# Three engines take the loop's instructions in the order of the source: an attention and feed-forward layer on one core

## The chip, the core and the metric

The kernel runs on one core of a Trainium2 chip. A core has a matrix engine (TensorE, PE in the profile; PEld is its weight load), a vector engine (VectorE, DVE), an activation engine (ScalarE, ACT), a general engine (GpSimd, POOL) and a queue that issues most transfers (SyncE, SP). Each engine takes its own instructions strictly in the order in which they stand in the built program, and waits at its head for what that instruction needs. The metric is the time of one execution in microseconds.

## The reference, cut to what matters

The input is 8 sequences of 1024 rows of width 256. Each goes through attention with 16 heads of 16, whose scores get a fixed band ("prior") added, then a layer norm, then a feed-forward part with ternary weights and a squared ReLU, then a second layer norm.

```python
scores = jnp.einsum('bhqd,bhkd->bhqk', Q, K) / math.sqrt(hd)
scores = scores + prior_lambda * _gaussian_mask(Lx)[None, None, :, :]
attn = jax.nn.softmax(scores, axis=-1)
out = jnp.einsum('bhqk,bhkd->bhqd', attn, V)
...
h = _bitlinear(x, w_fc) + gate * (x @ v.T @ fast_b.T @ u.T)
r = jnp.maximum(h, 0.0)
return _bitlinear(r * r, w_proj)
...
x = _layernorm(x + _L0_attn_ref(x, ...), axis=-1)
x = _layernorm(x + _L0_ffn_ref(x, ...), axis=-1)
```

All of it is in fp32; the queries and keys are split into two parts so that a faster fp32 form gives full precision.

## The kernel before

The heads are worked in groups of four. For each group the scores are computed twice: once with the queries on the partitions, to find each row's maximum (tiles `s`), and once with the keys on the partitions (tiles `e`), where the maxima, negated, come in as two more rows of the contraction. `exp` of `e` goes to SBUF, and a third product with the values gives the weighted sums (tile `av`).

The main loop has 512 turns, numbered by `g`, after 11 turns that only fill the pipeline. What one turn puts into the source, in this order:

- **E** (`exp_scores`, L437 to L462): two tiles `e`, each of two matmuls (L449), called E0 and E1 here. DVE adds the prior in place (L459) in the part of the tile that the band reaches; ACT takes `exp` (L461). Of each 8 turns in a row two have adds of 488 elements, two of 372, one of 116 and three have none.
- The second maximum that the turn before left over (`max_row`, L398 to L409: one DVE instruction over 1024 elements, L401).
- Every eighth turn `set_max` (L412 to L435): the maxima of a step are transposed on PE (`pmx`, L417), negated by two DVE instructions (`both`) and sent through DRAM into the query tiles, two turns before they are needed.
- **J**: two steps of the side work. Side jobs are Python generators in one queue (`jobs_of`, `run_job`): the projections of the next heads or the next sequence, the preparation of the weights, and the output projection and feed-forward part of the sequence before, in `chunk`s of 256 rows. A job hands control back at each `yield`.
- **S** (`max_scores`, L376 to L396): four matmuls for the scores 11 turns ahead. Tiles `s_0` and `s_1` are written alternately, one from the upper half of the array's rows and one from the lower half. DVE takes the maximum of `s_0` at once and that of `s_1` in the next turn.
- **AV** (`weigh`, L467 to L499): four matmuls with the `exp` of the turn before. Each has 17 output rows, in its own quarter of the array's columns. At the end of a step of 8 turns DVE and ACT copy `av` out (`avs`, L487, each taking two of the four heads) and it goes to DRAM; at the end of a sequence `normalize` (L502 to L521) reads the sums back, inverts them on DVE (L507) and scales.

The PSUM memory holds three tiles for `s` and `e` together (pool `ps_se`), one for `av`, and one, `misc`, for all side work. So E1 of a turn reuses the place of the `s_0` of the turn before; S needs the place of the turn's own E0 (free after its `exp`) and that of the `s_1` of the turn before (free after its maximum). Each side product must wait until the one before it has been taken out of `misc`: `ph` by ACT (`rl`, L591), `ptx1` by ACT (L574), `pk` and `pq` by ACT (`full`, L347), `po` and `py` by DVE (L562, L607), which then goes on with a layer norm (L523 to L541). In it POOL computes one small power (L532) for which DVE waits.

The order in the built program isn't that of the source. A scheduler takes the instructions at build time, prefers earlier source, and passes over what isn't ready by its own reckoning of durations: a matmul whose place in PSUM isn't free yet lets later ones pass. In the order built for the kernel before, the 2048 matmuls of AV stand in 913 groups with other matmuls between them (388 groups of one, 83 of two, 294 of three, 133 of four), those of S in 840 groups, of which 265 hold two of the upper half alone and 252 two of the lower half alone, and those of E in 833.

Of the kernel before, what the change touches and what calls it, by code (L numbers as in the profile page):

```python
# [10 lines left out]
F32 = mybir.dt.float32  # L11
# [5 lines left out]
P = 128  # L17
# [19 lines left out]
def tile_postln_layer(  # L37
# [20 lines left out]
    nc = tc.nc  # L58
    B, L, D = x.shape
# [19 lines left out]
    p1 = ctx.enter_context(tc.tile_pool(name="p1", bufs=1))  # L79
# [17 lines left out]
    def big(name):  # L97
        return epool.tile([P, 2 * HALF], F32, tag="e", name=name)
# [11 lines left out]
    for name, w in (("q", wq), ("k", wk), ("v", wv), ("o", wo)):  # L110
        t = big(f"raw_{name}")[:, : NDC * D].rearrange("p (c d) -> p c d", d=D)
# [4 lines left out]
    for name, src in (("q", bq), ("k", bk)):  # L116
        t = cpool.tile([P, NDC], F32, tag=f"b{name}", name=f"b{name}")
# [57 lines left out]
    for name in ("q", "k", "v"):  # L175
        t = cpool.tile([P, NDC, D], F32, tag=f"w{name}T", name=f"w{name}T")
# [20 lines left out]
    for s in range(SLOTS):  # L197
        for pr in range(NP):
            for a in range(2):
                for name in "qk":  # L200
                    t = cpool.tile(
                        [P, L], F32R, tag=f"{name}{s}{pr}{a}", name=f"st_{name}_{s}_{pr}_{a}"
                    )
# [7 lines left out]
    for n in range(2):  # L211
        t = cpool.tile([P, NB, NH, VW], F32, tag=f"v{n}", name=f"v_{n}")
# [7 lines left out]
    def ternary(w, n, name):  # L220

        sc = p2.tile([P, 3], F32, tag="sc", name=f"sc_{name}")
        t = big(f"tern_{name}")[:, :n]
        nc.vector.tensor_reduce(
            out=sc[:, 0:1], in_=w, axis=AX.X, op=ALU.add, apply_absolute_value=True
        )
        nc.vector.tensor_scalar(sc[:, 0:1], sc[:, 0:1], 1.0 / n, 1e-5, op0=ALU.mult, op1=ALU.max)
        nc.vector.tensor_scalar_mul(sc[:, 1:2], sc[:, 0:1], 0.5)  # L230
        nc.vector.tensor_scalar_mul(sc[:, 2:3], sc[:, 0:1], -0.5)
        nc.vector.tensor_scalar(t, w, sc[:, 1:2], None, op0=ALU.is_gt)
        nc.vector.scalar_tensor_tensor(
            out=t, in0=w, scalar=sc[:, 2:3], in1=t, op0=ALU.is_lt, op1=ALU.subtract
        )
        nc.vector.tensor_add(t, t, w)
        nc.vector.tensor_sub(t, w, t)
        nc.vector.tensor_scalar_mul(w, t, sc[:, 0:1])
# [3 lines left out]
    def prepare_fc(i):  # L242

        w = p1.tile([P, FF], F32, tag="rT", name=f"fc_{i}")[:, :D]
        nc.sync.dma_start(w, w_fc[ts(i, P), :])
        yield False
        ternary(w, D, f"fc_{i}")
        pu = misc(f"pu_{i}")
        nc.tensor.matmul(pu[:R, :P], u_sb[:, i, :], ident, start=True, stop=True)
        uT = p2.tile([R, P], F32, tag="uT", name=f"uT_{i}")  # L250
        nc.vector.tensor_copy(uT, pu[:R, :P])
        yield False
        pa = misc(f"pa_{i}")
        nc.tensor.matmul(pa[:R, :P], fb_sb, uT, start=True, stop=True)
        a = p2.tile([R, P], F32, tag="a", name=f"a_{i}")
        nc.vector.tensor_scalar_mul(a, pa[:R, :P], gate_c)
        yield False
        pw = misc(f"pw_{i}")
        for dc in range(NDC):
            nc.tensor.transpose(pw[:, ts(dc, P)], w[:, ts(dc, P)], ident)  # L260
        nc.vector.tensor_copy(wfT[:, :, ts(i, P)], pw[:, :D].rearrange("p (c h) -> p c h", h=P))
        yield False
        pl = misc(f"pl_{i}")
        for dc in range(NDC):
            nc.tensor.matmul(pl[:, ts(dc, P)], v_sb[:, ts(dc, P)], a, start=True, stop=True)
        nc.vector.tensor_add(
            wfT[:, :, ts(i, P)], wfT[:, :, ts(i, P)], pl[:, :D].rearrange("p (c h) -> p c h", h=P)
        )
        yield False

    def prepare_proj(i):
        w = p1.tile([P, FF], F32, tag="rT", name=f"proj_{i}")
        nc.sync.dma_start(w, w_proj[ts(i, P), :])
        yield False
        ternary(w, FF, f"proj_{i}")
        yield False
        for q in range(NHC // 4):
            pw = misc(f"pp_{i}_{q}")
            for c in range(4):
                nc.tensor.transpose(pw[:, ts(c, P)], w[:, ts(4 * q + c, P)], ident)  # L280
            nc.scalar.copy(wpT[:, ts(q, 4), ts(i, P)], pw.rearrange("p (c h) -> p c h", h=P))
            yield False
# [77 lines left out]
    def fill_stack(G):  # L360

        (b, g), s = divmod(G, NG), G % SLOTS
        for pr in range(NP):
            for a in range(2):
                at = P // 2 * a
                src = HD * ((g % 2) * HG + 2 * pr + a)
                for name in "kq":
                    nc.sync.dma_start(
                        stack[name, s, pr, a][at : at + P // 2].bitcast(F32),
                        parts_of[name, b, g // 2][src : src + HD].rearrange("p l n -> (p l) n"),  # L370
                    )
# [284 lines left out]
    for G in range(SLOTS):  # L656
        fill_stack(G)

    total = B * PER_B // 2
    opened, rest, es = False, None, {}  # L660
    for g in range(-LEAD, total + 1):
# [30 lines left out]
    for c in range(NCH):  # L692
        for _ in chunk(B - 1, c):
            pass


# [45 lines left out]
```

## Time and profile before

| what | value |
|---|---|
| median of 3 runs | 3170.52 us (3157.24 to 3173.5) |
| the profiled execution's own time | 3172.75 us |
| its span, first to last instruction | 3170.7 us |
| PE busy | 2984.8 us, 94% |
| DVE busy | 1912.3 us, 60% |
| ACT busy | 1237.8 us, 39% |
| first `exp` of the loop, end of the last | 99.2 us, 3020.7 us |
| mean granted TensorE clock | 0.950 |

The times are of one execution, taken by the hardware profiler. A line of a group reads: source line, engine, operation, output<-inputs, shapes, count, then the busy time and the mean length of one in ns, then the idle time of the engine before these instructions and what ended it. A line of the timeline reads: start and length in us, engine, line, operation, and how many equal ones followed each other; in brackets, how long the engine was idle before it and what released it. The busy time of PE is a union of lengths whose ends are modelled, so the start of one matmul to the start of the next tells more than the length. A line of the stages reads: stage, its length, then for each engine the busy time and the number of instructions, then the granted clock, the share of the transfer engines and GB/s. The clock in the profile's rows is either 1.00 or 0.50 at any one time; the mean says how the time divides.

From the first `exp` to the last the loop takes 2920 us, 5.70 us a turn. Some 99 us stand before it (loads, weights, the first projections and the first 11 turns of S) and 151 us after it (the last sequence's normalization and its four chunks).

### The profile page before, as it was taken

Reading aid. Unit: us, or ns where it says so; the run is one execution under the profiler, and the core shown is the slowest. Engines: PE = TensorE matmul, PEld = TensorE weight load, DVE = VectorE, ACT = ScalarE, POOL = GpSimd, SP = SyncE. Lnnn points to the kernel's source line nnn. Section 1 sums busy time; section 2 is a strip of 40 time slices with the busy share of each in tenths; the row PEclk is TensorE's granted clock in tenths of the full one; section 3 lists DMA queues with packets and bytes.
Section 4 is the critical chain, followed back from the end, with each engine's and each line's share of the span. In section 5 each row is a group of like instructions: output and inputs, shape, how many; then the busy total and the mean of one; then the engine's idle time right before and its main releaser. Section 6 shows DMA issues by size and latency. Waiting matters only on the chain.

```text
span 3170.7 us, 33164 instructions
## 1 busy us (share of the span) xinstructions
PE 2984.8 (94%) x11440; PEld 1311.8 (41%) x11440; DVE 1912.3 (60%) x3675; ACT 1237.8 (39%) x1417; POOL 407.3 (13%) x451
## 2 busy tenths in 40 slices
PE   4999999999999999999999999999999999999956
PEld 2333334444344443444344443444434444444335
DVE  3667675665666666566556656656665665666511
ACT  0323443443444444343444434444343434444410
POOL 4000101111110111101111111101111011111011
PEclk7867999999999998999999999999999999999978
DMA  5112322031312303122221312222031222202000
GB/s 152 58 36 54 105 52 77 24 98 43 92 51 52 91 23 98 37 88 68 58 64 29 106 43 79 64 52 87 24 102 37 78 71 51 80 21 52 12 23 14
DMA packets 106568, 193.89 MB, mean 61 GB/s; under 512 B 19264, under 2 KB 47952, under 8 KB 106400
## 3 DMA queue, kind: packets, MB, share of 16 engines
q1 hardware_dynamic: 104992, 190.38, 21.4%
q8 instruction: 90, 1.47, 0.2%
q10 hardware_dynamic: 1088, 1.05, 0.1%
q14 instruction: 78, 0.64, 0.1%
q0 software_dynamic: 320, 0.35, 0.1%
HBM read 105.73 MB, written 85.98 MB: 60 GB/s over the span
## 4 chain that ended last, share of the span: by engine, by line
PE 77%; issue 8%; DVE 7%; ACT 5%; DMA 2%; POOL 2%; SPq 0%; ACTq 0%; DVEq 0%; POOLq 0%
PE av L473 24%; PE e L449 16%; PE s L389 15%; PE ph L581 8%; PE py L598 6%; ACT exp L461 3%; DVE junk L401 3%; PE pk L336 2%; PE pv L309 2%; PE pq L336 2%; DVE e L459 1%; PE po L553 1%; DVE r L534 1%; ACT rl L591 1%; ACT avs L487 1%
## 5 line engine op out<-in xcount | busy, mean ns | idle before, releaser
L401 DVE CUSTOM_DVE_ANT_0 junk<-s,wide 128x1024 f32<-128x1024 f32 x1024 | 1249.6, 1220 | 718.3 <-PE s L389 688.5
L461 ACT ACTIVATE exp<-e 128x1024 f32<-128x1024 f32 x1024 | 1015.9, 1022 | 1285.0 <-DVE e L459 869.7
L473 PE MATMUL av<-exp,v 128*17 128x512 f32 x4096 | 1002.9, 615 | 0.2 <-ACT exp L461 0.2
L449 PE MATMUL e<-st_q,st_k 66*128 66x512 f32 (+1 forms) x2048 | 751.2, 465 | 17.0 <-ACT exp L461 9.2
L389 PE MATMUL s<-st_k,st_q 64*128 64x512 f32 x2048 | 654.3, 464 | 72.0 <-ACT exp L461 43.6
L449 PEld LDWEIGHTS e<-st_q,st_k 66*128 66x128 f32 (+1 forms) x2048 | 360.1, 195 | 514.0 <-issue 262.0
L389 PEld LDWEIGHTS s<-st_k,st_q 64*128 64x128 f32 x2048 | 269.0, 191 | 556.6 <-ACT exp L461 236.5
L459 DVE TENSOR_TENSOR e<-e,wide 128x372 f32<-128x372 f32 (+2 forms) x640 | 335.0, 543 | 248.1 <-PE e L449 242.7
L581 PE MATMUL ph<-x1T,wfT 128*128 128x256 f32 x1024 | 283.9, 411 | 13.8 <-ACT rl L591 9.4
L598 PE MATMUL py<-wpT,rT 128*128 128x256 f32 x1024 | 257.9, 386 | 3.0 <-ACT rl L591 3.0
L473 PEld LDWEIGHTS av<-exp,v 128*17 128x17 f32 x4096 | 114.9, 96 | 342.9 <-issue 324.0
L581 PEld LDWEIGHTS ph<-x1T,wfT 128*128 128x128 f32 x1024 | 197.5, 201 | 103.1 <-ACT rl L591 46.0
L598 PEld LDWEIGHTS py<-wpT,rT 128*128 128x128 f32 x1024 | 188.4, 189 | 80.1 <-issue 48.0
L592 POOL TENSOR_TENSOR rT<-rl 128x512 f32<-128x512 f32 x128 | 133.0, 1039 | 642.2 <-ACT rl L591 642.2
L487 ACT COPY avs<-av 17x512 f32<-17x512 f32 x128 | 73.9, 577 | 208.8 <-DVE avs L487 207.5
L591 ACT ACTIVATE rl<-ph 128x512 f32<-128x512 f32 x128 | 76.8, 600 | 156.8 <-PE ph L581 156.8
L487 DVE COPY avs<-av 17x512 f32<-17x512 f32 x128 | 87.4, 683 | 82.3 <-PE av L473 59.3
L532 POOL TENSOR_TENSOR rstd<-ve,mhalf 128x2 f32<-128x2 f32 x64 | 44.4, 694 | 599.4 <-DVE ve L530 599.4
L349 POOL CAST twok<-fullk 128x512 fp32r<-128x512 f32 x32 | 19.5, 610 | 616.3 <-ACT fullk L347 485.6
L553 PE MATMUL po<-woT,o 128*128 128x256 f32 x256 | 74.2, 399 | 21.9 <-POOL o L520 18.5
L520 POOL TENSOR_TENSOR o<-o,rec 128x512 f32<-128x512 f32 x32 | 40.5, 1285 | 409.5 <-DMA rec<-back 409.4
L548 POOL TENSOR_TENSOR x<-x,bo_row 128x256 f32<-128x256 f32 x64 | 45.8, 736 | 345.5 <-DMA x<-in_L_attn_x_dram 330.8
(109 smaller groups left out, 1100.6 us busy)
## 6 DMA issues: line engine op xcount, KB each, us to landing
parts_k<-twok SPq DMA_DIRECT2D x64, 512.0 KB
st_k<-parts_k SPq DMA_DIRECT2D x128, 256.0 KB
st_q<-parts_q SPq DMA_DIRECT2D x128, 256.0 KB
parts_q<-twoq SPq DMA_DIRECT2D x32, 512.0 KB
parts_q<-twoq SPq DMA_DIRECT2D x64, 256.0 KB
x<-in_L_attn_x_dram SPq DMA_DIRECT2D x16, 512.0 KB
x<-in_L_attn_x_dram SPq DMA_DIRECT2D x32, 256.0 KB
raw_o<-avs SPq DMA_DIRECT2D x256, 32.0 KB
```

The costliest lines, as they stand in the source:

```text
L336: nc.tensor.matmul(pt, wT[name][:, dc, ts(c, P)], xT[:, dc, ts(half, HALF)], start=(dc == 0), stop=(dc == NDC - 1),)
L389: nc.tensor.matmul(pair[a][:, kh, :], stack["q", s, pr, a][rows, ts(blk, P)], stack["k", s, pr, a][rows, ts(kh, HALF)], start=True, stop=True,
L401: nc.vector.tensor_tensor_reduce(out=junk, in0=t.rearrange("p k n -> p (k n)"), in1=wide[:, LEFT - P * blk : LEFT - P * blk + L], scale=1. ...
L449: nc.tensor.matmul(t[:, a, :], stack["k", s, pr, a][rows, ts(blk, P)], stack["q", s, pr, a][rows, ts(h, HALF)], start=True, stop=True,)
L459: nc.vector.tensor_add(part, part, add)
L461: nc.scalar.activation(e, t.rearrange("p a n -> p (a n)"), AF.Exp)
L473: nc.tensor.matmul(av_of[step][32 * j : 32 * j + HD + 1, :], v_bufs[b % 2][:, blk, g * HG + j, : HD + 1], es[j // 2][:, ts(j % 2, HALF)], ...
L487: (nc.scalar.copy if j % 2 else nc.vector.tensor_copy)(avs[rows], av[rows])
L581: nc.tensor.matmul(ph[:, ts(i, n)], wfT[:, dc, ts(2 * hp + i, P)], x1T[:, dc, :], start=(dc == 0), stop=(dc == NDC - 1),)
L591: nc.scalar.activation(rl, ph, AF.Relu)
L592: nc.gpsimd.tensor_mul(rT[:, ts(hp, 2), :].rearrange("p c n -> p (c n)"), rl, rl)
L598: nc.tensor.matmul(py[:, ts(i, D)], rT[:, hc, ts(i, P)], wpT[:, hc, :], start=(hc == 0), stop=(hc == NHC - 1),)
```

## The change

After the loop has been written, its instructions are gone through once more in the order of the source. Each instruction of PE, DVE or ACT gets a dependency on the instruction of the same engine before it. It carries no wait at run time; it only keeps the scheduler from placing one before the other. POOL and SP are left to the scheduler. The loop here is all from the first filling turn to the last chunk of the tail.

In addition the scratch tile of the weight preparation (`ternary`) is no longer taken from the pool of the four `exp` tiles but from the single scratch tile `junk`, which DVE's maxima write and nobody reads. The prior is added by DVE in both kernels.

```diff
@@ ternary
         sc = p2.tile([P, 3], F32, tag="sc", name=f"sc_{name}")
-        t = big(f"tern_{name}")[:, :n]
+        t = p1.tile([P, L], F32, tag="junk", name=f"tern_{name}")[:, :n]
@@ before the main loop
+    first = len(nc.cur_bb.bb.instructions)
     total = B * PER_B // 2
@@ after the last chunk
+    prev = {}
+    follow = mybir.DependencyInfo(mybir.DependencyClass.NoSync, mybir.DependencyReason.DATA)
+    for ins in list(nc.cur_bb.bb.instructions)[first:]:
+        if ins.engine in (nc.tensor.engine, nc.vector.engine, nc.scalar.engine):
+            if ins.engine in prev:
+                tc.add_manual_dep(ins, prev[ins.engine], follow, reason="order")
+            prev[ins.engine] = ins.name
```

In the built order of the changed kernel AV stands in 511 groups (510 of four), S in 503, always alternating between the halves, and E in 512 groups of four; a turn of a feed-forward chunk reads, on PE, "E0 E1, second half of `ph` 0, first half of `ph` 1, S, AV", and on ACT "`exp`, `exp`, `rl` 0".

## The prediction

> **What bounds the kernel now.** I read the page first, for the busy shares and the chain that ended last.
>
> ```profile
> span 3170.7 us, 33164 instructions
> PE 2984.8 (94%) x11440; PEld 1311.8 (41%) x11440; DVE 1912.3 (60%) x3675; ACT 1237.8 (39%) x1417; POOL 407.3 (13%) x451
> PE 77%; issue 8%; DVE 7%; ACT 5%; DMA 2%; POOL 2%; SPq 0%; ACTq 0%; DVEq 0%; POOLq 0%
> ```
>
> PE is the bound: it is on 77% of the chain. What fills it is told by the timeline of PE, in a stretch at full clock:
>
> ```profile
> 1000.97 0.81 PE L389 MATMUL s<-st_k,st_q 64*128 64x512 f32 x4
> 1001.70 1.04 PE L473 MATMUL av<-exp,v 128*17 128x512 f32 x4
> 1002.75 1.22 PE L449 MATMUL e<-st_q,st_k 66*128 66x512 f32 x4
> 1003.80 0.60 PE L294 MATMUL ptx<-ident,x 128*128 128x128 f32 x4
> 1005.30 0.73 PE L389 MATMUL s<-st_k,st_q 64*128 64x512 f32 x2
> 1005.96 1.03 PE L473 MATMUL av<-exp,v 128*17 128x512 f32 x2
> 1006.92 0.50 PE L389 MATMUL s<-st_k,st_q 64*128 64x512 f32 x1
> ```
>
> Take the distance from one start to the next. Four alternating S take 0.73 us (1000.97 to 1001.70), two of one half 0.66. An AV matmul counts as two records here: two heads take 1.05, one head alone 0.96. Over the trace a group of AV has a median of 0.96 to 0.98 us whether it holds one, two, three or four heads. So a group costs the same however full it is, and the 913 and 840 groups of the old order are what PE's time goes into.
>
> Next the groups by shape, for what DVE and ACT do in a turn:
>
> ```profile
> L401 DVE CUSTOM_DVE_ANT_0 junk<-s,wide 128x1024 f32<-128x1024 f32 x1024 | 1249.6, 1220 | 718.3 <-PE s L389 688.5 <-DVE pm L401 0.5
> L461 ACT ACTIVATE exp<-e 128x1024 f32<-128x1024 f32 x1024 | 1015.9, 1022 | 1285.0 <-DVE e L459 869.7 <-PE e L449 338.2 <-PE av L473 33.4
> L459 DVE TENSOR_TENSOR e<-e,wide 128x488 f32<-128x488 f32 x256 | 165.6, 670 | 155.5 <-PE e L449 154.8
> L459 DVE TENSOR_TENSOR e<-e,wide 128x372 f32<-128x372 f32 x256 | 136.4, 548 | 62.9 <-PE e L449 58.5 <-ACT fullk L347 3.3 <-issue 0.5
> L459 DVE TENSOR_TENSOR e<-e,wide 128x116 f32<-128x116 f32 x128 | 33.1, 279 | 29.8 <-PE e L449 29.3
> L591 ACT ACTIVATE rl<-ph 128x512 f32<-128x512 f32 x128 | 76.8, 600 | 156.8 <-PE ph L581 156.8
> ```
>
> DVE and ACT have room on average, and their idle time is spent waiting for PE. Whether they have room inside one turn is the question. The tail, where a chunk runs alone, shows the side work's own pace:
>
> ```profile
> 3057.13 3.78 PE L581 MATMUL ph<-x1T,wfT 128*128 128x256 f32 x8 [0.75 <-ACT rl L591]
> 3061.01 0.60 ACT L591 ACTIVATE rl<-ph 128x512 f32<-128x512 f32 x1 [3.93 <-PE ph L581]
> 3061.66 1.99 PE L581 MATMUL ph<-x1T,wfT 128*128 128x256 f32 x8 [0.75 <-ACT rl L591]
> 3071.61 0.69 DVE L607 TENSOR_TENSOR r<-py,x 128x512 f32<-128x512 f32 x1 [24.81 <-PE py L598]
> 3075.03 0.68 DVE L562 TENSOR_TENSOR r<-po,x 128x512 f32<-128x512 f32 x1
> ```
>
> A `ph` tile is 1.99 us at full clock, so half of it, one step of J, 1.0 (3.78 at half clock). The next one starts 0.05 after `rl` ends. A layer norm holds DVE for 3.42 (3071.61 to 3075.03), POOL's part included. Last, stages cut around one wait of PE, and the matmul that ended it:
>
> ```profile
> 1569.41:1572.82 3.41, 1.77 (x6) 0.70 (x5) 2.24 (x4) 2.49 (x4) 0.00 (x0) 1.00 1.04 237
> 1572.83:1593.30 20.47, 20.05 (x36) 5.48 (x36) 9.42 (x16) 5.37 (x6) 1.88 (x2) 0.50 0.35 103
> 1593.31:1603.50 10.19, 10.19 (x38) 3.69 (x36) 7.46 (x15) 3.95 (x5) 0.00 (x0) 1.00 0.06 19
> 1573.25 1.22 PE L389 MATMUL s<-st_k,st_q 64*128 64x512 f32 x2 [2.06 <-ACT exp L461]
> ```
>
> PE idled 2.06 us, then its clock stood at 0.50 for 20 us, in which it did as many matmuls as in 10 us at 1.00. Between 110 and 3000 us I find 16 idle gaps of PE of 1.33 us or more at full clock. After each the clock is halved within 4 us, for 3.4 to 20.5 us, about 10 on average.
>
> **What the change removes.** AV: 402 groups fewer at 0.98, 394 us. S: 337 fewer at 0.66, 222 us. E: a turn's pieces sum to 1.43 now, four in a row take 1.05, so 0.38 x 512 = 195 us. Together some 810 us of PE, 1.6 of the 5.7 us of a turn. This would be the gain if PE stayed the bound.
>
> **What it adds.** Now a turn is a chain through three engines. Count from the first matmul of E1; E0 began 0.53 before. After J, PE has S 0.73, AV 0.98 and the next E0 0.53: 2.24 until the next turn's E1. What matters is when S may start.
>
> - Plain turn, widest prior: E0's result is there at 0.25, two adds end at 1.50 (two in a row take 1.25 in the trace), the old `s_1` maximum at 2.75; only then has S its place. 2.75 + 2.24 = 5.0. With 372 it is 4.85, with 116 4.75, and with no prior J decides: 0.5 + 2 x 1.0 + 2.24 = 4.7. Without J and without prior 3.65.
> - Hand-over turn: J ends one `misc` tile and begins the next. ACT takes its instructions in source order, so `rl` stands behind both `exp`. Widest prior: first add ends 0.93, two `exp` in a row 1.94 (as the trace has them) to 2.9, `rl` to 3.5; PE idles from 1.5 to 3.5, then does 1.0 of `ph`, and S, AV and E0 are queued behind it: 4.5 + 2.24 = 6.75. With 372 6.6, with 116 6.35, with none 6.1. Where `pmx` comes between two tiles, there are two hand-overs, 1.0 more.
> - Layer-norm turn: DVE's 3.4 us stand between the maxima of `s_1` and `s_0`, and E1 of the next turn needs the latter: 2.75 + 3.42 + 1.30 + 0.05 = 7.5; with no prior 6.55.
>
> In the built order I count 155 plain turns with J (mean 4.82), 94 without (4.75), 181 hand-overs (6.28), 26 doubled ones (7.43) and 56 with a layer norm (7.18): 2926 us. To this come 64 copies of `av`: DVE 0.68, ACT 0.58, DVE 0.68, ACT 0.58 in a chain of 2.6, ahead of the next turn's adds and `exp`, 1.7 each, 109 us; and 7 ends of a sequence, where the inversion (L507) stands in DVE's order behind two round trips to DRAM (it waits 6.2 us at 3030 now), some 7.3 each, 51 us. The loop is 3086 against 2920 now: **+165 us at full clock**. PE's 810 us are given back to ACT's and DVE's order.
>
> Then the clock. 207 hand-overs, 56 layer norms and some 82 turns with a prior but no J leave PE idle for about 2 us each, 345 gaps, of the kind that halves the clock now. Not each can, since some fall while it is halved already, or are split between two of the clock's periods; I take 6 in 10, each costing half of the shortest stretch seen (3.4 us), 1.7 us of work on the path: **+352 us**. Bounds: none, and about 800, if the stretches last the 10 us they last now.
>
> **Weighed against a rule.** The Trainium skill ("TensorE: Matmul & The Clock Gate", section "Why this matters for your kernels") asks only for no idle gaps of PE over about 3 us. By that the 2 us gaps cost nothing and the sum would stop at +165; the 2.06 us row above speaks against it, so I go by the row.
>
> Costed at nothing: the scratch tile (one engine writes both uses, in order), the additions of V's bias and the two `both` (under 0.85 us, while DVE waits for S anyway; without that cover 0.6 to 0.85 on some 90 turns, 65 us, put in the range). Transfers: a group's stacks land 16 us after the first issue in the trace (1375 to 1391), and S needs them five turns later, 25 us or more; the maxima's way through DRAM takes 5 us of two turns. SP and POOL keep the scheduler's freedom. Start and tail already run in source order, at DVE's and ACT's pace: 0, within 15.
>
> Sum: 3172.75 (the profiled execution, 2 us over the median) + 165 + 352 = 3690.
>
> **Rivals.**
>
> - *No clock loss:* gaps of 2 us, one a turn and surrounded by denser matmuls, don't halve it. 3172.75 + 165 = 3340. For it: some gaps of 0.94 to 1.24 us leave the clock alone now. Against: the 16.
> - *The clock stays low:* at half clock a hand-over turn is about 9.9 us (ph, S, AV and E double), and two thirds of the loop run so: 3172.75 + 165 + 800 = 4140. For it: the 20 us row. Against: its S and AV were single; full groups load the array more, which may end a stretch sooner.
> - *Faster, PE's saving decides:* if hand-overs hide, say because the two `exp` come earlier than I set them, 207 turns fall from 6.4 to 4.8 and the clock stays up: 3340 - 335 = 3005. It decides from the point where a hand-over loses under 0.8 us instead of 1.6, with no halved clock. For it: 810 us of PE are really gone. Against: ACT's order is fixed and its two `exp` alone are 1.94.
> - *It doesn't do what it says:* excluded, the built order shows it.
>
> **How the numbers follow.** Likeliest case, 3450 to 3900: 0.50. No clock loss, 3200 to 3450: 0.19. Clock low, 3900 to 4250: 0.18. Faster, 2900 to 3155: 0.10. About even, since a chain summed from 512 turns can be off by 5%: 0.03. Leaving out the faster case and the top of the slow one, the range is 3230 to 4080. 0.5% is what a measurement of this kernel can tell: faster 0.10, same 0.03, slower 0.87.
>
> **What would show it.** AV in eights and S in fours in PE's timeline; PE idle before `ph`, released by `rl`, some 2 us each; ACT's `exp` and `rl` and DVE on far more of the chain than 12%; the mean clock down from 0.95 to about 0.8; DVE's and ACT's busy time unchanged. Wrong if PE's busy share stays above 90% at a clock of 0.95, or if the waits before `ph` are under 1 us.

## The result

The changed kernel takes 3560.0 us (median of four runs, 3551.62 to 3575.25); beside it on the same chip the kernel before took 3167.07 us. The ratio is 1.1249, with a 95% interval of 1.12 to 1.1299: 12.5% slower. The prediction was 3690 us, with a range of 3230 to 4080.

The page of the changed kernel, the lines that answer those shown of before:

```profile
span 3558.6 us, 33263 instructions
PE 2732.6 (77%) x11440; PEld 1309.8 (37%) x11440; DVE 1928.1 (54%) x3675; ACT 1213.7 (34%) x1417; POOL 407.9 (11%) x451
PE 55%; DVE 18%; ACT 11%; issue 8%; DMA 5%; POOL 2%; SPq 1%; DVEq 0%; ACTq 0%; POOLq 0%
```

PE has 252 us less to do than before (2984.8), and this although its mean granted clock fell from 0.950 to 0.834. It still carries the chain, but DVE and ACT now hold 29% of it instead of 12%, and they have done no more work: their busy times moved by 16 and 24 us. The span grew because engines wait for each other, and because the clock stood at half for longer.

The groups by shape (count | busy time, mean ns of one | idle time of the engine before them, and what ended it). First AV and S of the kernel before:

```profile
L473 PE MATMUL av<-exp,v 128*17 128x512 f32 x4096 | 1002.9, 615 | 0.2 <-ACT exp L461 0.2
L389 PE MATMUL s<-st_k,st_q 64*128 64x512 f32 x2048 | 654.3, 464 | 72.0 <-ACT exp L461 43.6 <-DMA st_q<-parts_q 17.4 <-DVE pm L401 9.3
```

Then the changed kernel:

```profile
L473 PE MATMUL av<-exp,v 128*17 128x512 f32 x4096 | 667.3, 728 | 1.8 <-ACT avs L487 1.6 <-ACT exp L461 0.2
L389 PE MATMUL s<-st_k,st_q 64*128 64x512 f32 x2048 | 557.7, 533 | 277.0 <-ACT exp L461 195.4 <-DVE pm L401 37.2 <-issue 22.5
L401 DVE CUSTOM_DVE_ANT_0 junk<-s,wide 128x1024 f32<-128x1024 f32 x1024 | 1250.5, 1221 | 870.4 <-PE s L389 842.8
L461 ACT ACTIVATE exp<-e 128x1024 f32<-128x1024 f32 x1024 | 997.5, 1021 | 1889.7 <-DVE e L459 1355.4 <-PE e L449 533.5
L459 DVE TENSOR_TENSOR e<-e,wide 128x488 f32<-128x488 f32 x256 | 163.5, 671 | 115.8 <-PE e L449 112.6
L459 DVE TENSOR_TENSOR e<-e,wide 128x372 f32<-128x372 f32 x256 | 134.2, 551 | 145.7 <-PE e L449 145.3
L591 ACT ACTIVATE rl<-ph 128x512 f32<-128x512 f32 x128 | 77.1, 602 | 46.6 <-PE ph L581 46.4
```

One instruction of DVE or ACT costs what it cost before (1221 and 1021 ns, before 1220 and 1022). The saving on PE is there: AV fell from 1002.9 to 667.3 us of busy time, S from 654.3 to 557.7. Against it stand the idle times: ahead of S alone PE idles 277.0 us, where it had 72.0; 195.4 of them end with ACT's `exp`, 37.2 with DVE's maxima. The waits of PE before the tile `ph`, and those of S (in all, times, longest):

```profile
PEld s L389 <- ACT exp L461: 290.3, 188, 14.7
PE s L389 <- ACT exp L461: 195.4, 124, 14.0
PEld ph L581 <- ACT rl L591: 149.8, 80, 3.0
PE ph L581 <- ACT rl L591: 115.8, 80, 2.6
```

A whole hand-over turn of the changed kernel, with 372 columns of prior, is in the timeline (start, duration, operation, idle time before it in brackets):

```profile
1431.10 1.21 PE L449 MATMUL e<-st_q,st_k 66*128 66x512 f32 x4
1431.94 1.01 DVE L459 TENSOR_TENSOR e<-e,wide 128x372 f32<-128x372 f32 x2 [0.50 <-PE e L449]
1432.14 1.02 PE L581 MATMUL ph<-x1T,wfT 128*128 128x256 f32 x4
1432.52 1.94 ACT L461 ACTIVATE exp<-e 128x1024 f32<-128x1024 f32 x2 [4.20 <-DVE e L459]
1432.86 1.21 DVE L401 CUSTOM_DVE_ANT_0 junk<-s,wide 128x1024 f32<-128x1024 f32 x1
1434.35 0.60 ACT L591 ACTIVATE rl<-ph 128x512 f32<-128x512 f32 x1
1435.01 1.13 PE L581 MATMUL ph<-x1T,wfT 128*128 128x256 f32 x4 [1.84 <-ACT rl L591]
1436.07 0.73 PE L389 MATMUL s<-st_k,st_q 64*128 64x512 f32 x4
1436.73 1.05 PE L473 MATMUL av<-exp,v 128*17 128x512 f32 x8
1437.71 1.19 PE L449 MATMUL e<-st_q,st_k 66*128 66x512 f32 x4
```

From E to E it is 6.61 us at full clock. The first half of J ends at 1433.16. Its `rl` has to wait for both `exp`, which wait for the additions; PE idles 1.84 us, and S, AV and the next E stand behind `ph`. AV is in eights and S in fours, as the order of the source has them.

Over the loop (first `exp` to last, 3312 us, before 2920 in the prediction's count) PE idles 716 us (before 87), and 32% of the time the clock stands at one half (before 7%).

### The profile page after: what moved, and what is told of

The parts are those of the page before. It is cut to its first block, busy times and chain, and to the rows that moved or that the text cites. A ratio compares the mean times of both kernels' runs of the same rounds, so it can differ in the third digit from the quotient of the medians.

```text
span 3558.6 us, 33263 instructions
## 1 busy us (share of the span) xinstructions
PE 2732.6 (77%) x11440; PEld 1309.8 (37%) x11440; DVE 1928.1 (54%) x3675; ACT 1213.7 (34%) x1417; POOL 407.9 (11%) x451
## 4 chain that ended last, share of the span: by engine, by line
PE 55%; DVE 18%; ACT 11%; issue 8%; DMA 5%; POOL 2%; SPq 1%; DVEq 0%; ACTq 0%; POOLq 0%
PE av L473 15%; PE e L449 13%; PE s L389 11%; DVE junk L401 7%; ACT exp L461 7%; PE ph L581 6%; PE py L598 5%; DVE e L459 4%; ACT rl L591 2%; DVE avs L487 2%; PE pk L336 1%; DMA den<-sums 1%; PE po L553 1%; DMA parts_q<-twoq 1%; ACT avs L487 1%
## 5 line engine op out<-in xcount | busy, mean ns | idle before, releaser
L401 DVE CUSTOM_DVE_ANT_0 junk<-s,wide 128x1024 f32<-128x1024 f32 x1024 | 1250.5, 1221 | 870.4 <-PE s L389 842.8
L461 ACT ACTIVATE exp<-e 128x1024 f32<-128x1024 f32 x1024 | 997.5, 1021 | 1889.7 <-DVE e L459 1355.4
L389 PE MATMUL s<-st_k,st_q 64*128 64x512 f32 x2048 | 557.7, 533 | 277.0 <-ACT exp L461 195.4
L449 PEld LDWEIGHTS e<-st_q,st_k 66*128 66x128 f32 (+1 forms) x2048 | 402.4, 223 | 739.8 <-issue 436.5
L473 PE MATMUL av<-exp,v 128*17 128x512 f32 x4096 | 667.3, 728 | 1.8 <-ACT avs L487 1.6
L389 PEld LDWEIGHTS s<-st_k,st_q 64*128 64x128 f32 x2048 | 228.7, 219 | 580.0 <-ACT exp L461 290.3
L581 PE MATMUL ph<-x1T,wfT 128*128 128x256 f32 x1024 | 317.6, 442 | 160.5 <-ACT rl L591 115.8
L581 PEld LDWEIGHTS ph<-x1T,wfT 128*128 128x128 f32 x1024 | 207.8, 214 | 238.0 <-ACT rl L591 149.8
L598 PE MATMUL py<-wpT,rT 128*128 128x256 f32 x1024 | 247.0, 382 | 31.1 <-ACT rl L591 21.1
L473 PEld LDWEIGHTS av<-exp,v 128*17 128x17 f32 x4096 | 71.4, 100 | 231.8 <-issue 227.7
L336 PE MATMUL pq<-xT,wqT 128*128 128x512 f32 x128 | 68.0, 616 | 36.0 <-ACT fullq L347 20.7
```

The costliest lines, as they stand in the source:

```text
L389: nc.tensor.matmul(pair[a][:, kh, :], stack["q", s, pr, a][rows, ts(blk, P)], stack["k", s, pr, a][rows, ts(kh, HALF)], start=True, stop=True,
L401: nc.vector.tensor_tensor_reduce(out=junk, in0=t.rearrange("p k n -> p (k n)"), in1=wide[:, LEFT - P * blk : LEFT - P * blk + L], scale=1. ...
L449: nc.tensor.matmul(t[:, a, :], stack["k", s, pr, a][rows, ts(blk, P)], stack["q", s, pr, a][rows, ts(h, HALF)], start=True, stop=True,)
L461: nc.scalar.activation(e, t.rearrange("p a n -> p (a n)"), AF.Exp)
L473: nc.tensor.matmul(av_of[step][32 * j : 32 * j + HD + 1, :], v_bufs[b % 2][:, blk, g * HG + j, : HD + 1], es[j // 2][:, ts(j % 2, HALF)], ...
L581: nc.tensor.matmul(ph[:, ts(i, n)], wfT[:, dc, ts(2 * hp + i, P)], x1T[:, dc, :], start=(dc == 0), stop=(dc == NDC - 1),)
```

## The experiments

All of them start from the changed kernel, and where a time is set against it by difference, mind that the kernel before, run beside each group of them, had medians from 3156.85 to 3175.18 us; the ratios are free of that. "PE alone in order" means that the loop that adds the dependencies takes only PE's instructions. A turn's price is from the start of one E to the next. PE's gaps are counted between the loop's matmuls, where they begin at full clock.

### Which engine's order costs the time

Four kernels change one line, the list of engines; `e1_pe_only` has PE alone:

```
-        if ins.engine in (nc.tensor.engine, nc.vector.engine, nc.scalar.engine):
+        if ins.engine in (nc.tensor.engine,):
```

> Only PE keeps the source order; DVE and ACT are left to the scheduler. Theory (the order of PE makes a turn one chain: hand-overs of the side tile stand before S): the same groups of AV and S as in the changed kernel, PE still idle before `ph` in most hand-over turns, since `rl` can only run once its `ph` is done and the two `exp` are ready about then; 3300 to 3560 us. Rival (ACT's order alone costs it, `rl` behind both `exp`): with ACT free `rl` goes first, the waits vanish and PE's 810 us are kept: 2900 to 3100 us.

`e2_dve_act` has DVE and ACT in order and leaves PE to the scheduler:

> DVE and ACT keep the source order, PE is left to the scheduler, so it may pass a side product that isn't ready. Theory: the loss goes with PE's order; PE is in pieces again and near its old bound, 3150 to 3300 us, clock above 0.92. Rival (the orders of DVE and ACT cost it): stays at 3450 to 3600 us.

`e5_pe_act` has PE and ACT, `e6_pe_dve` PE and DVE:

> PE and ACT keep the source order, DVE is left to the scheduler. After the first four runs the theory is: PE's order alone costs little (3199 us), and what the other two add is DVE's, which stands still at the end of a sequence (a turn of 18.8 us instead of 7.0) and behind the copies of `av`, and so lets PE's clock fall: 3200 to 3290 us. Rival: it is ACT's order (`rl` and the copies behind both `exp`): 3430 to 3560 us.

> PE and DVE keep the source order, ACT is left to the scheduler. Theory (DVE's order): 3430 to 3560 us. Rival (ACT's): 3200 to 3290 us.

| in order | us | ratio to before, 95% | clock | loop, us |
|---|---|---|---|---|
| none (before) | 3167 | 1 | 0.950 | 2920 |
| PE | 3198.59 | 1.0125 (1.0077 to 1.0172) | 0.895 | 2962 |
| PE, ACT | 3403.7 | 1.0732 (1.06 to 1.0864) | 0.869 | 3153 |
| PE, DVE | 3526.22 | 1.1118 (1.0986 to 1.1251) | 0.844 | 3282 |
| DVE, ACT | 3481.81 | 1.1021 (1.0914 to 1.1129) | 0.893 | 3217 |
| PE, DVE, ACT (after) | 3560.0 | 1.1249 (1.12 to 1.1299) | 0.834 | 3312 |

My theory, that the loss goes with PE's order, fell: with PE alone in order nearly all of it is gone (below the 3300 I had set, but above the rival's 3100), and with PE left free and the two others in order most of it stays, as the rival had it. The third run fell between its two expectations, the fourth into the theory's. Left free, PE has to do its small groups again (884 of AV, busy 3117.8 us, 90% of the span), and it idles 244 us of the loop, where it idled 87 in the kernel before. The scratch tile has moved in all of these kernels but the first, and was not tried alone. On top of PE's order, DVE's costs some 330 us and ACT's some 205, both together only 361, so a part of what they cost must lie in the same places. The same turn with PE alone in order shows where:

```profile
1282.05 1.22 PE L449 MATMUL e<-st_q,st_k 66*128 66x512 f32 x4
1282.55 1.23 DVE L401 CUSTOM_DVE_ANT_0 junk<-s,wide 128x1024 f32<-128x1024 f32 x1
1283.70 1.00 DVE L459 TENSOR_TENSOR e<-e,wide 128x372 f32<-128x372 f32 x2
1284.17 0.60 ACT L591 ACTIVATE rl<-ph 128x512 f32<-128x512 f32 x1 [4.88 <-PE ph L581]
1284.66 1.94 ACT L461 ACTIVATE exp<-e 128x1024 f32<-128x1024 f32 x2
1284.82 1.13 PE L581 MATMUL ph<-x1T,wfT 128*128 128x256 f32 x4 [0.69 <-ACT rl L591]
1287.52 1.21 PE L449 MATMUL e<-st_q,st_k 66*128 66x512 f32 x4
```

The scheduler takes DVE's old maximum of `s_1` ahead of the additions, and `rl` ahead of the two `exp`. PE idles 0.69 us instead of 1.84, and the turn is 5.47 us instead of 6.61. It takes both exchanges: at full clock a hand-over turn with 372 columns takes 6.67 to 7.18 us with PE and ACT in order, and 6.62 with PE and DVE. The hand-over turns without a prior stay at 6.02 in both kernels, those with 116 columns at 6.36 and 6.35.

That PE alone in order is no faster than the kernel before, though PE is busy 2585.7 us instead of 2984.8, is put down here to what is left of the chain: hand-overs of 5.5 to 6.4 us, and half clock for 19% of the loop. `e8_pe_one_tile` below tests the first.

### The exchange written into the source

If that is the cause, a kernel with all three engines in order must win by it too. `e9_order` keeps every engine in order, and PE's order as it was; it writes the old maximum ahead of the additions, and the two `exp` behind the first step of J (what `exp_of` and `waiting` hold is left out here):

```
         if 0 <= g < total:
-            es[g] = [exp_scores(i) for i in (now, now + 1)]
+            ts_of = [exp_scores(i) for i in (now, now + 1)]
         if rest is not None:
             max_row(*rest)
             rest = None
+        while waiting:
+            part, add = waiting.pop(0)
+            nc.vector.tensor_add(part, part, add)
...
             if g >= 0:
                 opened = run_job(now)
+            if 0 <= g < total:
+                es[g] = [exp_of(now + a, t) for a, t in enumerate(ts_of)]
```

> All three engines stay in the order of the source, and the order itself is written differently: DVE takes the old maximum of s_1 ahead of the turn's additions, and ACT takes the first step of J (rl and its like) ahead of the two exp. PE's order is the same as after. Theory (the loss is what stands ahead of what in DVE's and ACT's order, not that the order is fixed): a hand-over turn with a prior falls from 6.4-6.7 to about 5.5 us, one without from 6.02 to about 5.5, as in the kernel with PE alone in order; 181 hand-overs x 0.9 and 26 doubled ones x 1.0 are about 190 us, plus up to 100 of clock: 3270 to 3390. Rival (a fixed order loses because no turn can choose any more; what the hand-overs gain, the plain turns lose, whose exp come 1.2 us later): 3480 to 3620.

Measured: 3324.4 us, ratio 1.0518 (1.0478 to 1.0558), clock 0.873, loop 3064. That is 236 us less than after, inside the theory's 3270 to 3390. The timeline of `e9_order` at the same place:

```profile
1323.53 1.20 PE L449 MATMUL e<-st_q,st_k 66*128 66x512 f32 x4
1324.03 1.22 DVE L401 CUSTOM_DVE_ANT_0 junk<-s,wide 128x1024 f32<-128x1024 f32 x1
1325.18 1.00 DVE L681 TENSOR_TENSOR e<-e,wide 128x372 f32<-128x372 f32 x2
1325.63 0.60 ACT L596 ACTIVATE rl<-ph 128x512 f32<-128x512 f32 x1 [3.02 <-PE ph L586]
1326.12 1.94 ACT L466 ACTIVATE exp<-e 128x1024 f32<-128x1024 f32 x2
1326.28 1.13 PE L586 MATMUL ph<-x1T,wfT 128*128 128x256 f32 x4 [0.69 <-ACT rl L596]
1328.98 1.20 PE L449 MATMUL e<-st_q,st_k 66*128 66x512 f32 x4
```

5.45 us, the scheduler's turn reproduced to 0.02. At full clock a hand-over turn goes from 6.74, 6.62, 6.02 us (488, 372 and no columns of prior) to 5.52, 5.47, 5.53; a doubled one with 488 columns from 7.76 to 6.55. So a good part of the loss, 236 of 393 us, is not that the order is fixed but what stands ahead of what in it. What `e9_order` still has over PE alone in order, 102 us of loop, comes mostly from the ends of sequences and the copies of `av`: the turn that ends a sequence takes 19.8 us there against 6.8, and one with the four copies beside 488 columns of prior 6.8 to 7.0 against 5.19. Some of that is won back by its hand-overs without a prior, 5.53 against 6.02.

### Hand-overs taken away

`e3_one_tile` leaves all three in order, and from the second sequence on a turn begins no second tile of J:

```
-        if g >= 0:
-            opened = run_job(now)
+        if g >= 0 and (opened or now < PER_B):
+            opened = run_job(now)
```

Besides, the new maxima (`set_max`) are set at the end of a turn, and one empty step behind the first layer norm is left out. That leaves 73 of the 207 hand-overs. By the trace two tiles of J meet ahead of S in 16 turns, all in the first sequence; in the rest it is the maxima's transpose that follows a side tile, behind S and AV.

> All three engines in source order, but from the second sequence on a turn ends its side work when it has closed its tile in `misc`, so that two tiles meet in one turn only 73 times instead of 207 (the maxima's transpose moves to the end of the turn before, one empty step of a chunk goes). Theory (hand-overs cost 1.6 us each at full clock and then the halved clock): turns by the classes sum to 2686 + 160 us instead of 2926 + 160, a gain of 240 us, and about 130 fewer idle gaps, 100 us more: 3180 to 3280 us, clock about 0.88. Rival (the chain of DVE's maxima sets the time, hand-overs lie beside it): 3480 to 3580 us.

Measured: 3243.54 us, ratio 1.0267 (1.0194 to 1.034): 316 us less than after, inside the theory's 3180 to 3280. Most of the former hand-over turns are at 4.5 to 4.95 us. But the theory's 100 us from the clock are not in it: expected was a clock of about 0.88, the trace has 0.820, and 1041 us of the loop at half clock against 1073. The gain is time at the turns themselves. `e8_pe_one_tile` is the same with PE alone in order:

> PE alone in source order, and one side tile a turn as in the run with one tile. Theory: in the run with PE alone the 181 hand-over turns still take 6.70 us against 4.87 of plain ones; removing 130 of them takes 200 to 280 us off its 3199: 2920 to 3000 us, 5 to 8% faster than the kernel before. Rival (the time goes to another wait, DVE's layer norms or the transfers): 3120 us or more.

Measured: 2970.24 us, ratio 0.9365 (0.926 to 0.9471). **This is 6.4% faster than the kernel before**, and in it PE's saving is collected: PE is busy 2546.2 us, against 2984.8 in the kernel before. One tile a turn with all engines left to the scheduler wasn't run, so what that rule alone would bring is not shown. The timeline of one of its turns, again with 372 columns:

```profile
1198.84 1.21 PE L449 MATMUL e<-st_q,st_k 66*128 66x512 f32 x4
1199.88 1.89 PE L580 MATMUL ph<-x1T,wfT 128*128 128x256 f32 x8
1201.70 0.98 PE L389 MATMUL s<-st_k,st_q 64*128 64x512 f32 x4
1202.61 1.05 PE L473 MATMUL av<-exp,v 128*17 128x512 f32 x8
1202.70 0.60 ACT L590 ACTIVATE rl<-ph 128x512 f32<-128x512 f32 x1
1203.59 1.21 PE L449 MATMUL e<-st_q,st_k 66*128 66x512 f32 x4
```

Both halves of `ph` run in one go, `rl` comes behind the `exp` without anyone waiting for it, PE has no gap, and the turn takes 4.75 us.

### The end of a sequence

In the timeline of the changed kernel, the turn in which a sequence ends:

```profile
1352.56 0.55 DVE L507 RECIPROCAL den<-den 128x64 f32<-128x64 f32 x1
1363.98 0.55 DVE L507 RECIPROCAL den<-den 128x64 f32<-128x64 f32 x1 [10.87 <-DMA den<-sums]
1364.57 1.25 DVE L459 TENSOR_TENSOR e<-e,wide 128x488 f32<-128x488 f32 x2
1365.33 1.94 ACT L461 ACTIVATE exp<-e 128x1024 f32<-128x1024 f32 x2 [12.19 <-DVE e L459]
1366.41 1.80 PE L389 MATMUL s<-st_k,st_q 64*128 64x512 f32 x4 [13.95 <-ACT exp L461]
```

DVE stands 10.87 us before the second reciprocal, whose operand is on its way through DRAM, with the additions queued behind it, ACT behind these, and PE idle for 13.95 us. `e7_late_inverse` starts the loads where they were and does the reciprocals and what follows three turns later (the lines that take them up again are left out here):

```
-            for c in range(NDC):
-                normalize(b, c)
+            late.append([LATE, b, [load_sums(b, c) for c in range(NDC)]])
```

> The changed kernel, all three engines in source order, but the two inversions at the end of a sequence, with what follows from them, stand three turns later in the source; the loads of the sums stay where they are. Theory: seven turns of 18.8 us lose their 12 us, and the 40 to 50 us of halved clock after each, which cost some 15 more: 160 to 230 us less than the changed kernel, 3330 to 3400 us. Rival (these waits lie beside other waits): 3480 us or more.

Measured: 3482.31 us, ratio 1.098 (1.0859 to 1.1101). The turn falls from 18.9 to 7.73 us, 78 us over seven ends, and so does the time. By its number this is the rival's range, 3480 or more, though the wait itself did cost what it lasted; the theory had hoped for more, because it took the stall for what halves the clock in the turns around it. Those turns stay at 6.9 us, at half clock, without the stall. What they have in common is that they have no J.

### Filling the turns without J

`e4_filler` adds work: in about 94 turns without J, PE does two idle matmuls of 512 columns whose result nobody reads.

```
+        if g >= 0 and not running and not (jobs and jobs[0][0] <= now):
+            idle = misc(f"idle_{g}")
+            for n in range(2):
+                nc.tensor.matmul(idle, ident, wT["q"].rearrange("p c d -> p (c d)"), start=True, stop=True)
```

> The changed kernel with more work: in the 84 or so turns of the loop in which no side job is due, two idle matmuls of 512 columns into `misc`, about 1.9 us of PE at full clock, in the time in which PE waits there now. Theory (idle PE halves its clock; these turns take 7.1 us at a share of 0.71 of halved clock instead of 4.75): 100 to 200 us less than the changed kernel, 3360 to 3460 us, clock 0.87 or more. Rival (the clock follows something else, or costs nothing there): no less than 3560 us, up to 3720 if the added 160 us of PE count in full.

Measured: 3491.27 us, ratio 1.1051 (1.1004 to 1.1098). More work, 69 us less: the clock rises from 0.834 to 0.891, the share of the loop at half clock falls from 0.323 to 0.196, and a turn without J and with 372 columns takes 4.68 us (median), where it took 6.84. The time at half clock within the filled turns falls from some 490 to some 140 us. The size was missed by 31 us, the direction was the theory's. On the fastest kernel the same filler is `e11_pe_one_filler`:

> PE alone in order, one tile of J a turn (e8_pe_one_tile, 2970 us), plus two idle matmuls of 512 columns, whose result nobody reads, in the turns that have no J. Theory (turns without J let the clock be halved; 0.206 of that kernel's loop is at half clock): the time falls to 2900-2960 though PE does more. Rival (with one tile a turn few turns lack J, or the matmuls cost what the clock brings): 2965 to 3030.

Measured: 2965.06 us, ratio 0.938 (0.9341 to 0.9419), so no difference from `e8_pe_one_tile`. The clock did rise, from 0.888 to 0.920; what it brings and what the idle matmuls cost come out about even (PE's busy time is 2587.5 us against 2546.2). The result is at the lower edge of the rival's range.

### All three in order, as well as I can write it

`e10_order_late_one` joins the edits of `e9_order`, `e3_one_tile` and `e7_late_inverse`, with all engines in order.

> The order of e9_order, all three engines in order, with one tile of J a turn from the second sequence on (as in e3_one_tile) and the inversion three turns later (as in e7_late_inverse). Theory: e3_one_tile's 3244 less 77 us for the seven ends of a sequence and about 65 for its 73 remaining hand-overs: 3050 to 3140, below the kernel before with no freedom left to DVE and ACT. Rival (fixed DVE and ACT lose to the scheduler whatever the order): above 3180.

Measured: 3193.71 us, ratio 1.0096 (1.0062 to 1.013), above the theory's 3050 to 3140 and in the rival's range. The parts don't add up, and the timeline of `e10_order_late_one` shows one reason:

```profile
1247.53 2.48 POOL L531 TENSOR_TENSOR o<-o,rec 128x512 f32<-128x512 f32 x2 [6.96 <-DMA rec<-back]
1249.95 0.61 POOL L349 CAST twok<-fullk 128x512 fp32r<-128x512 f32 x1
1251.94 0.69 ACT L347 ACTIVATE fullq<-pq,bq 128x512 f32<-128x512 f32 x1 [7.83 <-POOL twok L350]
1252.52 1.93 ACT L466 ACTIVATE exp<-e 128x1024 f32<-128x1024 f32 x2
1252.67 3.78 PE L336 MATMUL pq<-xT,wqT 128*128 128x512 f32 x4 [5.57 <-ACT fullq L347]
```

The inversion is later by three turns, and POOL's product with `rec` now stands ahead of the `twok` that the projection of the next sequence needs. ACT's `fullq` waits 7.83 us for that POOL work, and since J's step now stands ahead of the `exp`, both `exp` wait behind it. The turn of that stall, the eighth of a sequence, takes 12.9 to 14.9 us in seven sequences, where it took 4.5 to 4.8 in `e3_one_tile`: 65 us, of the 54 to 144 that are missing. What the new order of ACT could win was also small here, since one tile a turn leaves few hand-overs. Without that collision the kernel would be at about 3130 (an estimate: 3194 less 65); it wasn't run. That would still be 160 us above PE alone in order with one tile a turn (2970). So the rival, that a fixed order of DVE and ACT loses to the scheduler whatever the order, is not refuted; no kernel here has all three in order and is faster than the kernel before.

## Why the prediction was right or wrong

The sign held, and so did the place and the mechanism at full clock; the way to the clock's share did not. The likeliest case, 3450 to 3900, is the one that came. The sum was 130 us too high. Point by point:

**What the change removes.** PE's saving is real: without DVE's and ACT's order and with nearly no hand-overs it carries the kernel to 0.9365 of before (`e8_pe_one_tile`). That it is given back to ACT's and DVE's order, and not to PE's, is shown by the four kernels that fix one or two engines, against the theory with which I went into them.

**Hand-over turns.** "`rl` stands behind both `exp`" was right, and shown by writing it the other way round (`e9_order`). The prices were right within 0.1 us: at full clock 6.74, 6.62, 6.36 and 6.02 us, predicted 6.75, 6.6, 6.35 and 6.1; doubled with 488 columns 7.76, predicted 7.75. What I did not see is that the widths of the prior matter only through the place of the additions in DVE's order, ahead of the old maximum. I noted the order and priced it, but not that exchanging the two would be worth a microsecond a turn.

**Plain turns.** 4.50 to 4.92 us at full clock, predicted 4.7 to 5.0: about 25 us less over 155 turns.

**Turns without J.** At full clock 4.68 with 372 columns (in `e4_filler`), predicted 4.75 as the mean of all. As the kernel runs they take 7.11 on average, for the clock, as told below.

**Layer norms.** The 56 turns sum to 335 us, predicted 402, but some of it falls into the next turn (hand-over turns behind one take 8.5 to 11.3 us, partly at half clock). Some 17 us too much, by an estimate from these turns.

**Copies of `av`.** 1.1 to 1.5 us each at full clock, predicted 1.7: 25 us too much. **Ends of a sequence.** 11 us each by `e7_late_inverse`, predicted 7.3: 26 us too little, since DVE waits 10.87 us there and not 6.2.

**The loop at full clock.** With the measured prices on the counted turns the terms are lower by 25 (plain), 36 (without J, of whom the last 11 have no S), 16 (hand-overs), 17 and 25, and higher by 26: 93 us in all, so about 2990 instead of 3086. The rest of the measured 3312, about 320, is the clock's share by this working; an estimate, not a measurement.

**The clock.** 352 us predicted, about 320 by that remainder: the term came out nearly right, but the way to it was wrong, so that the two lie close is luck. I set 345 gaps, 6 in 10 of them halving the clock for 3.4 us, 207 halvings. The trace has 108 stretches at half clock, of 9.7 us on average (47.8 at the longest). Half as many, three times as long. And they don't stand where I put them: of 1073 us at half clock 537 lie in the 93 turns without J, 391 in 181 hand-over turns. Of the gaps of 1.33 us and more that end with `rl`, the hand-over's own, 14 of 56 are followed by half clock; of those that end with DVE's maxima, 21 of them in the turn behind a layer norm, 27 of 29 are. And where the clock is at half when turns without J come, it stays there: the seven stretches of 47.8 us run from the last turns of one sequence into the first of the next, where there is no J. So the hand-overs, to which I gave most of the term, were the wrong places to look for what halves the clock, though much of the half clock falls on them; layer norms and the turns without J, which I gave the rest, did more. Two runs bear this out: take the hand-overs away, and the time at half clock stays (1041 us in `e3_one_tile`); fill the turns without J, and its share falls by 0.127 (`e4_filler`).

**Weighed against a rule.** The Trainium skill ("TensorE: Matmul & The Clock Gate", section "Why this matters for your kernels") asks for no idle gap of PE over about 3 us between bursts. In the changed kernel 3 of the gaps that begin at full clock are longer, while the clock goes to half 108 times in the loop; the rows decide against the rule as a bound. But the row that I went by said too much in turn: of 165 gaps of 1.33 us or more 70 are followed by half clock within 4 us (in the kernel before, counted in the same way, 13 of 14, so that "after each" has an exception there too).

**The rivals.** *No clock loss* (3340) and *the clock stays low* (4140) enclose the result. *Faster* hung on the hand-overs' hiding and gave 3005; with nearly no hand-overs and DVE and ACT left to the scheduler that is what happens (2970 in `e8_pe_one_tile`), in another kernel than this one.

**Signs named.** AV in eights and S in fours, PE idle before `ph` by `rl` (1.84 us in the turn shown, 1.45 on average over 80), chain of DVE and ACT 29% instead of 12, clock 0.834 (expected about 0.8), busy times of DVE and ACT nearly unchanged: all there. The start moved by 4 us, the tail by 1.

## What to carry to other kernels

Here a fixed order over several engines turned each turn of the loop into one chain, so count the chain through all engines and not the busy times: the price is set by what stands just ahead of an instruction that another engine waits for (here `rl` behind two `exp`), and two exchanges in the source, one on DVE and one on ACT, were worth 236 of 393 us. Fix the order only on the engine where it saves work, leave the engines with room to the scheduler, and take away the waits that order alone can't hide (here the hand-over from one PSUM tile to the next within a turn). When a delayed piece of work is moved, look up what comes behind it on every queue that it passes: the inversion moved off DVE came to stand in ACT's way by way of POOL.

## What the runs showed of the hardware beyond that

- The length of an idle gap says much about the clock that follows, but not all. In the changed kernel, of gaps that began at full clock, 28 of 28 of 2.2 us or more were followed by half clock within 4 us, 4 of 4 between 2.0 and 2.2, and 38 of 133 between 1.33 and 2.0. In `e1_pe_only` it is 18 of 20 from 2.2 up and 32 of 87 between 1.33 and 2.0. But in `e3_one_tile` all 18 gaps between 1.33 and 2.0 were followed by it, and in `e8_pe_one_tile` 21 of 28, so a short gap can go either way; what decides it is not shown. In the changed kernel, of 14 gaps of 1.8 to 1.9 us that ended with `rl`, one was followed by half clock.
- Half clock can last: a turn without J that takes 4.7 us at full clock (`e4_filler`) takes 6.9 at half. In the stretches of 47.8 us, each with the long wait at the end of a sequence in it, PE is busy for 62 to 64% of the time.
- Idle matmuls brought 69 us where the clock was at half for a third of the loop (`e4_filler`), and nothing where it was for a fifth (`e11_pe_one_filler`), though the mean clock rose in both.
